# The middle of a mixture-of-slots layer on one core: the norm of the second half re-ordered, and attention pieces set between two halves of a tile

## The chip, the core and the metric

The kernel runs on one core of a Trainium2 chip. The core has a matrix engine (TensorE, PE in the profile; its weight loads are the row PEld), VectorE (DVE), ScalarE (ACT), GpSimd (POOL) and SyncE (SP), whose queue issues most of the DMAs. The metric is the time of one launch in microseconds (us), lower is better, as the median over several runs. All arithmetic is in float32; one float32 matmul of the program is two instructions on PE.

## The reference, cut to what matters

The input x is 4096 tokens of 256 values. Four layers follow one another, each with a layer norm ahead and a residual sum behind: causal attention with 16 heads (a), a soft mixture of experts, another causal attention (b), and the same mixture again with the same weights. The change is in the mixture, which is run twice:

```python
logits = (jnp.einsum('tzd,ed->tze', x, phi_w) + phi_b).reshape(t, z, n, p)  # 64 experts, 32 slots
D = jax.nn.softmax(logits, axis=3)       # over the slots of an expert
C = jax.nn.softmax(logits, axis=2)       # over the experts
X_tilde = jnp.einsum('tznp,tzd->npd', D, x)          # 2048 slots of 256 values
X_tilde = jnp.clip(X_tilde, -33000.0, 65000.0)
mu = jnp.mean(X_tilde, axis=-1, keepdims=True)
var = jnp.mean(jnp.square(X_tilde - mu), axis=-1, keepdims=True)
X_tilde = (X_tilde - mu) * jax.lax.rsqrt(var + LN_EPS)
X_tilde = jnp.tanh(X_tilde)
Y_tilde = jnp.einsum('npd,ndH->npH', X_tilde, expert_w) + expert_b[:, None, :]
Y = jnp.einsum('tznp,npH->tzH', C, Y_tilde)
```

## The kernel before

A mixture layer (`_Experts.run`) has three stages.

**The sweeps.** The 2048 slots are cut into two halves h = 0 and 1 of 1024, and each half sweeps over the 32 token tiles t of 128 tokens, 64 steps in all. A step computes the logits two steps ahead (`logits`: matmuls into the PSUM buffers `lg`, of which there are three, the sum with the bias on DVE at L786, the maximum at L791, a subtraction on POOL at L794, the exponential on ACT at L797), divides one step ahead by the sum of the exponentials (`divide`: a reduction on DVE at L807, a reciprocal at L808, a product on POOL at L809) and adds eight PE instructions into four PSUM banks `acc`. At the end of a half the four banks are clipped into `xt` (DVE, L985). The raw logits go to DRAM (`ld`), for the third stage.

**The norm and the experts of a half.** Groups of 512 slots, numbered n = 0 to 3 (0 and 1 are the first half, 2 and 3 the second), pass three steps. `centre` gets the mean with four PE instructions in one PSUM bank, subtracts it on DVE (two instructions, L701) and squares on ACT (L703). `spread` gets the variance with 16 PE instructions, its root on ACT (L716), and on DVE a reciprocal (L717) and a diagonal matrix (L718). `squash` multiplies with two PE instructions and two on DVE (L730), and takes the tanh on ACT (L731). `product(ec)` then multiplies 128 slots with their experts' weights (16 PE instructions) and adds the bias on DVE (L743); ec = 0 to 7 is the first half, 8 to 15 the second. All these use `net.bank()`, one PSUM bank in this layer. For the first half the steps are hung beside the second half's sweep (`net.beside` runs one of the queue `net.side` per call). For the second half nothing is left to hang them beside: they stand between the sweeps and the combination, written out by hand.

**The combination.** For each tile t the softmax over the experts is needed with the slots on the partitions. `load_l` brings the logits back, `begin` computes the exponentials (POOL L826, ACT L829), `quarter` or `sums` their sum on DVE (four reductions, L856, or one, L845) and `inverse` the reciprocal, with a copy on ACT (L841). `turn_r` transposes the reciprocals on PE and copies them out on ACT (L872, the tile `r`); `turn` transposes the exponentials on PE, 16 transposes in four PSUM buffers' worth, each scaled by `r` on DVE into `lT` (L884). `weigh(t, lo, hi)` is the matmul with the experts' results `ys`, two PE instructions for each ec of the range, 32 for a full tile. `ended` adds the residual (DVE, L901). The tiles 0 and 1 are begun in the last steps of the sweeps (the table `ahead`, by step) and turned there. In the first mixture layer, pieces of attention b's projections (scalings of x on ACT, transposes, matmuls with an ACT copy at L172 and a DVE subtraction at L173) are called with `net.beside(3)` at the end of an iteration, from t = 7 on. At the end of t = 2 attention b's weights are fetched by DMAs from ACT's queue, and at the end of t = 6 and 10 `net.roots` takes a root on ACT (L99) for the norm of the next four tiles.

**What sets the order.** PE instructions stand in the order of the program. On the other engines a list scheduler of the language places an instruction when its own model finds it ready, except where it is wrapped in `pin` (`tc.keep_in_program_order`): that puts it behind the one instruction that was written just before it on its engine. If that one is itself free, the pinned one can move up with it. DMAs of this layer on the SP queue are pinned too. Every engine then works through its stream in order.

Weights: `load_w(ec)` fetches 1 MB of expert weights; 8 to 10 and 14, 15 go to three buffers, 11, 12, 13 to the views 1, 2, 0 of `net.zone`, which the sweeps have used until then (view 0 holds the exponentials of tile 0). `load_b(1)` fetches the second half's bias into the buffer `ebt`, which holds the exponentials of tile 1 until they are turned.

Of the kernel before, what the change touches and what calls it, by code (L numbers as in the profile page):

```python
# [10 lines left out]
F32 = mybir.dt.float32  # L11
# [8 lines left out]
P = 128  # L20
# [22 lines left out]
class _Net:  # L43
# [28 lines left out]
    def bank(self):  # L72
        return self.banks.tile([P, 512], F32, name="bank")
# [533 lines left out]
class _Experts:  # L607
# [28 lines left out]
    def run(self):  # L636
# [10 lines left out]
        with ExitStack() as ctx:  # L647
# [44 lines left out]
            wview = lambda k: net.zone[:, ts(k, E)].rearrange("p (n c h) -> p n c h", n=4, c=2)  # L692
            sqs = {}

            def centre(n):
                xs = xt[:, :, ts(n, 512)]
                mu = net.bank()
                for d in range(2):
                    mm(mu, mean, xs[:, d, :], start=d == 0, stop=d == 1)
                for d in range(2):  # L700
                    nc.vector.tensor_tensor(xs[:, d, :], xs[:, d, :], mu, ALU.subtract)  # L701
# [4 lines left out]
            def spread(n):  # L706
                sq = sqs[n]
                var = net.bank()
# [7 lines left out]
                nc.scalar.activation(r, var[:, 0:4], AF.Sqrt, bias=net.eps)  # L716
                nc.vector.reciprocal(r, r)  # L717
                nc.vector.tensor_tensor(  # L718
                    sq[:, 0, :].rearrange("p (k e) -> p k e", k=4),
                    _bc(net.ident.unsqueeze(1), [P, 4, P]), _bc(r.unsqueeze(2), [P, 4, P]),  # L720
                    ALU.mult,
                )


            def squash(n):
                xs = xt[:, :, ts(n, 512)]
                rs = net.bank()
                mm(rs, one, sqs[n][:, 0, :], start=True, stop=True)
                for d in range(2):
                    nc.vector.tensor_tensor(xs[:, d, :], xs[:, d, :], rs, ALU.mult)  # L730
                nc.scalar.activation(xs, xs, AF.Tanh)  # L731

            def product(ec, bank=net.bank):
                w = ews.pop(ec)
                y = bank()[:, 0:D]
                for j in range(4):
                    for c in range(2):
                        mm(
                            y[ds(32 * j, 32), :], xt[:, c, ds(ec * P + 32 * j, 32)],
                            w[:, j, c, :], start=c == 0, stop=c == 1,  # L740
                        )
                h, e = ec // NC2, ec % NC2
                nc.vector.tensor_tensor(ys[h][:, e, :], y, ebs[h][:, e, :], ALU.add)  # L743
                if ec < NC2:
                    load_w(ec + 3)

# [187 lines left out]
            for k in range(8):  # L934
                ahead[21 + k] = lambda k=k: quarter(k // 4, k % 4)
            ahead[29] = lambda: [maxima(t) for t in range(2, 4)]
            logits(*seq[0])
            logits(*seq[1])
            divide(*seq[0])
            for n, (h, t) in enumerate(seq):  # L940
                if t == 0:
                    acc = [
                        [pa.tile([P, 512], F32, name=f"acc{d}{n2}") for n2 in range(2)]
                        for d in range(2)
                    ]
                if n + 2 < len(seq):
                    logits(*seq[n + 2])
                if n + 1 < len(seq):
                    divide(*seq[n + 1])
                if n < len(seq) - 2:  # L950
                    net.beside(3)
                else:
                    assert not net.side and not net.urgent and not net.agenda
                if h == 1 and t in ahead:
                    ahead[t]()
                if n == len(seq) - 2:

                    nctx.close()
                    pools["lT"] = pool("fc_t", 2)
                    pools["l"] = pool("fc_l", 1)  # L960
                    pools["e"] = pool("fc_w", 1)
                    load_l(2)
                    turn_r(0, first)
                    turn(0, first)
                    begin(2)
                    for k in range(3):
                        load_w(NC2 + 3 + k, wview((1, 2, 0)[k]))
                    load_l(3)
                if n == len(seq) - 1:
                    turn_r(1, first)  # L970
                    turn(1, first)
                    load_b(1)
                ef = es.pop((h, t)).rearrange("p n s -> p (n s)")
                for n2 in range(2):
                    for d in range(2):
                        mm(
                            acc[d][n2], x[:, t, ts(d, P)], ef[:, ts(n2, 512)],
                            start=t == 0, stop=t == NT - 1,
                        )
                if h == 0:  # L980
                    net.beside(3)
                if t == NT - 1:
                    for n2 in range(2):
                        for d in range(2):
                            nc.vector.tensor_scalar(  # L985
                                xt[:, d, ds(h * EH + n2 * 512, 512)], acc[d][n2],
                                -33000.0, 65000.0, ALU.max, ALU.min,
                            )
# [14 lines left out]
            pools["t"] = pool("fc_p", 3, space=PSUM)  # L1003
            pools["o"] = pool("fc_o", 2, space=PSUM)
            two = pool("fc_x", 1, space=PSUM)
            weigh(0, 0, NC2)
            centre(2)
            centre(3)
            spread(2)
            spread(3)  # L1010
            weigh(1, 0, NC2)
            squash(2)
            squash(3)
            for ec in range(NC2, NEC):
                product(ec, (net.bank, lambda: two.tile([P, 512], F32, name="bank2"))[ec % 2])
                if ec < NC2 + 2:
                    load_w(ec + 6)
                if ec < NC2 + 4:
                    quarter(2, ec - NC2)
            turn_r(2)  # L1020
            begin(3)
            rctx.close()
            pools["e"] = pool("fc_w2", 3, side="right")
            pools["l"] = pool("fc_l2", 2, side="right")
# [1 line left out]
            for t in range(NT):  # L1026
                if t + 4 < NT:
                    load_l(t + 4)
                if t > 0:
                    ended(t - 1)  # L1030
                    if t + 3 < NT:
                        begin(t + 3)
                if t == 0:
                    weigh(0, NC2, NEC)
                if 2 <= t + 1 < NT:
                    turn(t + 1)
                if t > 0 and out is None:
                    net.stats(t - 1)
                if t + 4 < NT:
                    maxima(t + 4)  # L1040
                if 4 <= t + 2 < NT:
                    sums(t + 2)
                if t > 0:
                    weigh(t, NC2 if t == 1 else 0, NEC)
                if 4 <= t + 2 < NT:
                    turn_r(t + 2)
                if t == 0:
                    sums(3)
                    turn_r(3)
# [107 lines left out]
```

## Time and profile before

| | |
|---|---|
| median of 3 runs | 5242.63 us (5239.64 to 5249.16) |
| profiled execution, its time | 5241.35 us |
| profiled execution, its span | 5239.3 us |
| mean granted clock of PE | 0.982 |
| first mixture layer in the trace | its last sweep product ends near 2296 us, its combination runs to 2654 us |
| second mixture layer in the trace | its last sweep product ends near 4915 us, its combination runs to the end of the span |

Times are microseconds from the start of the span. A timeline row gives start, duration, engine, line, operation, what it writes and reads, the count of instructions merged in the row, and in brackets how long the engine sat idle before the row and what ended that. A row of stretches gives, for a stretch, its length, the busy time of the engines with their counts, then the granted PE clock (1.00 is full speed), the busy share of the DMA engines and the GB/s they moved.

### The profile page before, as it was taken

The numbers are of one execution on the slowest core, as the hardware profiler recorded it, in microseconds if no ns is written. First come the engines' busy times: TensorE is split into PE (matmuls) and PEld (weight loads), VectorE is DVE, ScalarE is ACT, GpSimd is POOL, SyncE is SP. The second block draws the span as 40 slices with busy tenths as digits, with TensorE's granted clock in tenths as the row PEclk, the third lists the DMA queues.
The fourth block names the chain that finished last, engine by engine and source line by source line (L and its number), as shares of the span: only waits on it lengthen the run. The fifth ranks groups of instructions, "written<-read, shape, count | busy, mean of one in ns | idle before, by whom it ended". The sixth has DMA issues, their size and how long they took to land.

```text
span 5239.3 us, 79442 instructions
## 1 busy us (share of the span) xinstructions
PE 5025.7 (96%) x29936; PEld 2683.4 (51%) x29936; DVE 4141.6 (79%) x7790; ACT 2633.1 (50%) x3108; POOL 1157.2 (22%) x1084
## 2 busy tenths in 40 slices
PE   7999999999999999989989999999999999999899
PEld 4444454445455344447754444545444553444488
DVE  5688989898989388767756889888889893787687
ACT  3466676766667622113224666766666676211132
POOL 3211100000000255534412111000000002555353
PEclk8999999999999999999999999999999999999999
DMA  6433222121121013433444332222121210134343
GB/s 252 140 107 127 67 73 68 61 67 61 59 64 53 32 78 104 148 127 114 144 175 144 107 127 67 72 68 64 64 64 57 64 53 31 77 105 147 122 148 111
DMA packets 266160, 499.16 MB, mean 95 GB/s; under 512 B 44944, under 2 KB 109968, under 8 KB 258096
## 3 DMA queue, kind: packets, MB, share of 16 engines
q1 hardware_dynamic: 260544, 485.57, 28.0%
q10 hardware_dynamic: 4896, 7.87, 0.4%
q8 instruction: 235, 3.85, 0.3%
q14 instruction: 149, 1.22, 0.1%
q0 software_dynamic: 336, 0.66, 0.1%
HBM read 336.73 MB, written 156.76 MB: 94 GB/s over the span
## 4 chain that ended last, share of the span: by engine, by line
PE 75%; DVE 11%; POOL 5%; issue 3%; ACT 3%; DMA 2%; SPq 0%; DVEq 0%; POOLq 0%; ACTq 0%
PE o L67 26%; PE bank L67 22%; PE sc L67 17%; PE acc L67 4%; DVE mx L386 4%; PE lg L67 4%; DVE junk L380 2%; POOL e L794 2%; PE ps L70 2%; POOL e L809 2%; ACT e L797 1%; DVE l L786 1%; ACT pb L462 1%; POOL e L826 1%; DMA zone<-ld 0%
## 5 line engine op out<-in xcount | busy, mean ns | idle before, releaser
L462 ACT ACTIVATE pb<-sc 128x1024 f32<-128x1024 f32 (+3 forms) x2304 | 2070.1, 950 | 1104.0 <-PE sc L67 1101.3
L386 DVE TENSOR_REDUCE mx<-bank 128x1 f32<-128x512 f32 x3584 | 2225.4, 682 | 179.5 <-PE bank L67 174.8
L67 PE MATMUL bank<-k,q 64*128 64x512 f32 (+3 forms) x4608 | 1354.7, 454 | 71.0 <-DVE mx L386 29.8
L67 PEld LDWEIGHTS bank<-k,q 64*128 64x128 f32 x4608 | 669.4, 186 | 1178.1 <-DVE mx L386 777.6
L67 PE MATMUL o<-pb,va 128*32 128x512 f32 (+3 forms) x9216 | 1160.4, 575 | 3.1 <-POOL pb L466 2.8
L67 PE MATMUL sc<-q,k 64*128 64x512 f32 (+3 forms) x4608 | 991.9, 391 | 9.6 <-ACT pb L462 9.2
L67 PE MATMUL sc<-qm,one 64*128 64x512 f32 (+3 forms) x4608 | 951.8, 378 | 0.0
L466 POOL TENSOR_SCALAR_AFFINE_SELECT pb<-pb 128x256 f32<-128x256 f32 x512 | 204.8, 407 | 2281.3 <-ACT pb L462 2275.5
L380 DVE CUSTOM_DVE_ANT_0 junk<-bank,maskw 128x128 bf16<-128x128 f32 (+3 forms) x1024 | 502.5, 491 | 258.9 <-PE bank L67 150.6
L67 PEld LDWEIGHTS sc<-q,k 64*128 64x128 f32 x4608 | 512.2, 187 | 138.2 <-ACT pb L462 98.9
L67 PEld LDWEIGHTS sc<-qm,one 64*128 64x128 f32 x4608 | 528.9, 187 | 67.7
L67 PE MATMUL acc<-e,x 128*128 128x512 f32 x1024 | 473.1, 605 | 19.3 <-POOL e L809 14.7
L797 ACT ACTIVATE e<-e 128x1024 f32<-128x1024 f32 x128 | 135.2, 1057 | 694.6 <-POOL e L794 694.6
L67 PE MATMUL lg<-zone,xnT 128*128 128x512 f32 x1024 | 463.3, 594 | 4.4 <-DVE l L786 3.8
L67 PE MATMUL o<-ys,lT 128*128 128x256 f32 x2048 | 464.9, 386 | 1.6 <-DVE xt L985 1.6
L67 PEld LDWEIGHTS o<-ys,lT 128*128 128x128 f32 x2048 | 392.6, 194 | 56.1 <-DVE xt L985 3.2
L826 POOL TENSOR_TENSOR e<-l,mc 128x1024 f32<-128x1024 f32 x120 | 281.3, 2365 | 319.5 <-DMA l<-ld 209.9
L67 PEld LDWEIGHTS o<-pb,va 128*32 128x32 f32 x9216 | 183.2, 108 | 290.6 <-issue 265.7
L67 PEld LDWEIGHTS acc<-e,x 128*128 128x128 f32 x1024 | 192.6, 193 | 265.5 <-issue 215.9
L809 POOL TENSOR_TENSOR e<-e,s 128x1024 f32<-128x1024 f32 x128 | 244.8, 1912 | 370.0 <-DVE s L808 348.5
L67 PEld LDWEIGHTS lg<-zone,xnT 128*128 128x128 f32 x1024 | 192.2, 190 | 245.7 <-issue 217.9
L807 DVE TENSOR_REDUCE s<-e 128x32 f32<-128x1024 f32 x128 | 156.1, 1219 | 155.2 <-ACT e L797 154.6
(122 smaller groups left out, 3208.4 us busy)
## 6 DMA issues: line engine op xcount, KB each, us to landing
k<-ak SPq DMA_DIRECT2D x144, 512.0 KB
k<-bk SPq DMA_DIRECT2D x144, 512.0 KB
ld<-l SPq DMA_DIRECT2D x128, 512.0 KB
l<-ld SPq DMA_DIRECT2D x60, 1024.0 KB
w<-in_L_ffn_expert_w_dram SPq DMA_DIRECT2D x26, 1024.0 KB
q<-aq SPq DMA_DIRECT2D x32, 512.0 KB
rb<-dd SPq DMA_DIRECT2D x64, 256.0 KB
q<-bq SPq DMA_DIRECT2D x32, 512.0 KB
```

The lines of the kernel that those rows point to most:

```text
L67: self.tc.keep_in_program_order(self.nc.tensor.matmul(*a, **k))
L70: self.tc.keep_in_program_order(self.nc.tensor.transpose(o, i, self.ident))
L380: nc.vector.tensor_tensor_reduce(out=junk[:, 0:w], in0=scs[h2][:, 0:w], in1=maskw[:, QB - w : QB], scale=1.0, scalar=-3e38, op0=ALU.add, o ...
L386: nc.vector.tensor_reduce(m, scs[h2], AX.X, ALU.max)
L462: nc.scalar.activation(pb[:, :, off:QB], sc[:, :, off:QB], AF.Exp)
L466: nc.gpsimd.affine_select(out=d, in_=d, compare_op=ALU.is_ge, fill=0.0, base=0, pattern=[[0, 2], [1, P]], channel_multiplier=-1,)
L786: nc.vector.tensor_tensor(lf[:, ts(n, 512)], lg, phb[:, ds(h * EH + n * 512, 512)], ALU.add)
L794: nc.gpsimd.tensor_tensor(e, l, _bc(m.unsqueeze(2), [P, NH, SLOT]), ALU.subtract)
L797: nc.scalar.activation(ef, ef, AF.Exp)
L807: nc.vector.tensor_reduce(s, e, AX.X, ALU.add)
L809: nc.gpsimd.tensor_tensor(e, e, _bc(s.unsqueeze(2), [P, NH, SLOT]), ALU.mult)
L826: nc.gpsimd.tensor_tensor(e[:, ns, :], l, _bc(cms[t].unsqueeze(1), [P, NH, SLOT]), ALU.subtract)
```

## The change

It has five parts. (1) `centre`, `spread` and `squash` take the PSUM bank as an argument, and their DVE instructions, those of `product` and the clipping L985 are pinned. (2) `turn_r(0)` and `turn_r(1)` move up into the sweep, to its steps t = 26 and 30 of the second half; the transposes of the tiles 0 and 1 move down, out of the last two steps. (3) Behind the sweeps, the two groups of the second half are taken side by side, group 2 in the one bank and group 3 in a second bank that before only the products used in turn, with `turn(1)` between `centre` and `spread`, `turn(0)` between `spread` and `squash`, and `weigh(0, 0, 8)` behind `squash`; the weights and the bias that need the freed buffers are fetched behind those steps. (4) `begin(3)` moves from behind the products to ahead of them, and `weigh(1, 0, 8)` is cut in four pieces between pairs of products. (5) In the combination a tile's `weigh` is cut in two halves, and from t = 7 on in the first mixture layer `net.beside(3)` is called between the halves and not at the iteration's end.

```diff
-            def centre(n):
+            def centre(n, bank=net.bank):
                 xs = xt[:, :, ts(n, 512)]
-                mu = net.bank()
+                mu = bank()
...
-                    nc.vector.tensor_tensor(xs[:, d, :], xs[:, d, :], mu, ALU.subtract)
+                    pin(nc.vector.tensor_tensor(xs[:, d, :], xs[:, d, :], mu, ALU.subtract))
...
-                nc.vector.tensor_tensor(ys[h][:, e, :], y, ebs[h][:, e, :], ALU.add)
+                pin(nc.vector.tensor_tensor(ys[h][:, e, :], y, ebs[h][:, e, :], ALU.add))
...
             ahead[29] = lambda: [maxima(t) for t in range(2, 4)]
+            ahead[26] = lambda: (quarter(1, 1), turn_r(0, first))
+            ahead[30] = lambda: turn_r(1, first)
...
                     load_l(2)
-                    turn_r(0, first)
-                    turn(0, first)
                     begin(2)
-                    for k in range(3):
-                        load_w(NC2 + 3 + k, wview((1, 2, 0)[k]))
-                    load_l(3)
-                if n == len(seq) - 1:
-                    turn_r(1, first)
-                    turn(1, first)
-                    load_b(1)
+                    for k in range(2):
+                        load_w(NC2 + 3 + k, wview(1 + k))
...
             two = pool("fc_x", 1, space=PSUM)
+            load_l(3)
+            banks = (net.bank, lambda: two.tile([P, 512], F32, name="bank2"))
+            centre(2, banks[0])
+            centre(3, banks[1])
+            turn(1)
+            load_b(1)
+            spread(2, banks[0])
+            spread(3, banks[1])
+            turn(0)
+            load_w(NC2 + 5, wview(0))
+            squash(2, banks[0])
+            squash(3, banks[1])
+            begin(3)
             weigh(0, 0, NC2)
-            centre(2)
-            centre(3)
-            spread(2)
-            spread(3)
-            weigh(1, 0, NC2)
-            squash(2)
-            squash(3)
             for ec in range(NC2, NEC):
-                product(ec, (net.bank, lambda: two.tile([P, 512], F32, name="bank2"))[ec % 2])
+                product(ec, banks[ec % 2])
                 if ec < NC2 + 2:
                     load_w(ec + 6)
                 if ec < NC2 + 4:
                     quarter(2, ec - NC2)
+                if ec % 2:
+                    weigh(1, ec - NC2 - 1, ec - NC2 + 1)
             turn_r(2)
-            begin(3)
...
+                beside = self.attention is not None and t > 6
                 if t > 0:
-                    weigh(t, NC2 if t == 1 else 0, NEC)
+                    lo = NC2 if t == 1 else 0
+                    half = lo + (NEC - lo) // 2
+                    weigh(t, lo, half)
+                    if beside:
+                        net.beside(3)
+                    weigh(t, half, NEC)
                 if 4 <= t + 2 < NT:
                     turn_r(t + 2)
...
-                    if t > 6:
-                        net.beside(3)
```

More of the change, by code (lines that the diff above doesn't have):

```diff
@@ L700, in centre, with spread @@
                 for d in range(2):
-                    nc.vector.tensor_tensor(xs[:, d, :], xs[:, d, :], mu, ALU.subtract)
+                    pin(nc.vector.tensor_tensor(xs[:, d, :], xs[:, d, :], mu, ALU.subtract))
                 sqs[n] = ewk.tile([P, 2, 512], F32, name="sq")
                 nc.scalar.activation(sqs[n], xs, AF.Square)
-            def spread(n):
+            def spread(n, bank=net.bank):
                 sq = sqs[n]
-                var = net.bank()
+                var = bank()
                 for k in range(4):
@@ L716, in spread @@
                 nc.scalar.activation(r, var[:, 0:4], AF.Sqrt, bias=net.eps)
-                nc.vector.reciprocal(r, r)
-                nc.vector.tensor_tensor(
+                pin(nc.vector.reciprocal(r, r))
+                pin(nc.vector.tensor_tensor(
                     sq[:, 0, :].rearrange("p (k e) -> p k e", k=4),
@@ L721, in spread, with squash @@
                     ALU.mult,
-                )
-            def squash(n):
+                ))
+            def squash(n, bank=net.bank):
                 xs = xt[:, :, ts(n, 512)]
-                rs = net.bank()
+                rs = bank()
                 mm(rs, one, sqs[n][:, 0, :], start=True, stop=True)
                 for d in range(2):
-                    nc.vector.tensor_tensor(xs[:, d, :], xs[:, d, :], rs, ALU.mult)
+                    pin(nc.vector.tensor_tensor(xs[:, d, :], xs[:, d, :], rs, ALU.mult))
                 nc.scalar.activation(xs, xs, AF.Tanh)
@@ L984, in run @@
                         for d in range(2):
-                            nc.vector.tensor_scalar(
+                            pin(nc.vector.tensor_scalar(
                                 xt[:, d, ds(h * EH + n2 * 512, 512)], acc[d][n2],
                                 -33000.0, 65000.0, ALU.max, ALU.min,
-                            )
+                            ))
                     if h == 0:
```

## The prediction

> **What bounds the kernel now.** I read the page's first part, the stretches around the two mixture layers, and the engines' timelines there. PE is busy in 96% of the span, so only what shortens PE's work, its waits or its slow clock counts.
>
> ```profile
> PE 5025.7 (96%) x29936; PEld 2683.4 (51%) x29936; DVE 4141.6 (79%) x7790; ACT 2633.1 (50%) x3108; POOL 1157.2 (22%) x1084
> 2357.50:2653.90 296.40, 274.16 (x1436) 236.00 (x1437) 211.69 (x286) 80.83 (x129) 118.89 (x51) 0.98 0.34 115
> 4962.19:5239.30 277.11, 273.86 (x1485) 240.52 (x1484) 206.73 (x234) 75.24 (x113) 130.45 (x56) 0.99 0.40 131
> 2273.39:2342.82 69.43, 49.73 (x272) 31.32 (x270) 33.72 (x53) 14.46 (x20) 18.12 (x9) 0.83 0.48 153
> 4893.60:4962.02 68.42, 47.97 (x272) 30.84 (x270) 33.62 (x52) 14.69 (x20) 15.77 (x8) 0.85 0.46 143
> ```
>
> The last two rows are the passage from sweep to combination (end of the third-last sweep product to `turn_r(3)`): PE is idle for some 20 us of each, with a granted clock of 0.83 to 0.85. The second row, the second layer's combination, is full; the first layer's lacks 22 us. The PE timeline of the second passage names the waits:
>
> ```profile
> 4901.77 1.12 PE L70 MATMUL lg<-ident,zone 128*128 128x128 f32 x4 [3.63 <-ACT r L872]
> 4904.71 5.10 PE L67 MATMUL acc<-e,x 128*128 128x512 f32 x8
> 4911.70 3.60 PE L67 MATMUL acc<-e,x 128*128 128x512 f32 x8
> 4922.90 1.99 PE L67 MATMUL bank<-xt,mean 128*128 128x512 f32 x4 [1.38 <-DVE xt L701]
> 4928.93 3.58 PE L67 MATMUL bank<-mean,sq 128*128 128x1 f32 x16 [0.66 <-ACT rx L716]
> 4932.37 6.70 PE L67 MATMUL o<-ys,lT 128*128 128x256 f32 x16
> 4953.91 1.09 PE L67 MATMUL bank<-w,xt 128*32 128x256 f32 x16 [1.87 <-DMA w<-in_L_ffn_expert_w_dram]
> 4962.02 0.33 PE L70 MATMUL rT<-ident,s 128*128 128x128 f32 x1 [3.31 <-ACT s L841]
> ```
>
> Step by step one bank serves both groups, so group 3 waits for group 2's DVE work; and 6.70 us for sixteen instructions that take 3.72 elsewhere is PE at half clock after waits. In the first layer's combination (PE, then ACT):
>
> ```profile
> 2425.41 0.65 PE L70 MATMUL ps<-ident,e 128*128 128x128 f32 x4 [4.32 <-DVE lT L884]
> 2425.90 8.76 PE L67 MATMUL o<-ys,lT 128*128 128x256 f32 x32
> 2517.14 0.66 PE L70 MATMUL ps<-ident,e 128*128 128x128 f32 x4 [1.02 <-DVE lT L884]
> 2464.33 1.06 ACT L829 ACTIVATE e<-e 128x1024 f32<-128x1024 f32 x1 [1.26 <-POOL e L826]
> 2465.29 0.25 ACT L872 COPY r<-rT 128x128 f32<-128x128 f32 x1
> ```
>
> The copy of `r` for tile t+1 stands behind exponentials of tile t+3 that are late, DVE cannot scale, PE waits. 9.13 us is an undisturbed iteration (2381.68 to 2390.82).
>
> **The passage, step by step.** Removed from the last two sweep steps: 32 transposes and two `turn_r`. `acc` of t = 31 then waits only for its divided exponentials: L809 starts at 4903.35 and takes 1.91, so 4905.26 and not 4911.70, a gain of 6.4 (first layer 2285.04 against 2292.58, 7.5). PE idles ahead of t = 30's `acc` (free at 4893.6 plus `turn_r(1)`, data at 4898.48); that is no loss, as the chain through DVE, POOL and ACT sets 4905.26.
>
> From there to `turn_r(3)` PE must do: `acc` 3.44; two `centre` 3.44; 32 transposes 3.9; two `spread` 3.8; two `squash` 1.72; `weigh(0)`'s first half 3.45; eight products at 1.02, 8.2; `weigh(1)`'s four pieces 3.45; `turn_r(2)` 0.1; `weigh(0)`'s second half 3.45. Sum 35.0. What is still waited for, by laying DVE's pinned order beside it (clips 0.7 each behind `acc`, two subtractions 1.28 per group, four scalings 2.5 per tile, 1.0 per `spread`, 1.28 per `squash`): the fourth transposes of each tile need a scaling first, 0.7 and 0.8; a product waits 0.3 for its bank; `turn_r(3)` waits 1.0 for `sums(3)` (3.6 plus 0.35 plus the copy, from the last bias sum on, beside 3.45 of `weigh`). Sum 2.8. The ACT steps hide: squares (1.06 each) under `turn(1)`, roots and a table load (1.28) under `spread(3)` and `turn(0)`, both tanh under `weigh(0)`; uncovered, tanh would cost 2.1. So 37.8, against 50.3 (4911.70 to 4962.02) and 50.2: gains of 12.5 and 12.4.
>
> In the second layer `turn(2)` behind this runs at a slow clock (3.47 for 2.1 us of transposes), 1.5 more. **Passages: 6.4 + 12.5 + 1.5 + 7.5 + 12.4 = 40.3.**
>
> Moved at no cost: `begin(3)`. Its exponentials wait today behind `turn_r(2)`'s copy on ACT, hence the 3.31; placed ahead of the products, POOL has 4.7 us of work some 10 us early. Its SP loads keep their order except that the weights of ec = 13 go behind `load_l(3)` and `load_b(1)`; the product needs them some 11 us after they are issued, and the pair of 1 MB loads behind product 9 landed within 5.9 and 8.9 us (4945.01 issued, 4950.9 and 4953.9 used). The same pair has 7.5 and 8.3 us in the new order: 0 to 1.5 us a layer, I take 0.
>
> `turn_r(0)` in the sweep holds an `lg` buffer until its ACT copy, which is pinned behind t = 28's exponential: 13 us with two buffers in place of three. PE then waits some 2.1 us at the next logits, but the sweep's period of 7.97 there is set by the DVE-POOL-ACT chain (PE works 6.9 of it), and the evictions come 7 us after the matmuls. Cost 0; at most 2.1 a layer.
>
> The pins on the first half's steps: those DVE rows already stand behind L808 of their step (L701 at 2062.69 after L808 at 2062.42). 0.
>
> **The combination of the first layer.** Four matmul pieces (t = 17 to 20) make iterations of 11.73; their PE work is 1.72, so 0.87 each is the DVE subtraction ahead of the scalings; between the halves it lies under 3.45 us of `weigh`: 3.5. Three transposes' pieces wait 0.42, 0.58, 0.59 where 0.15 is normal: 1.1. The piece at t = 31 spares the 1.40 that the next one waits for its bank. The order of the pins matters more: the exponentials of `begin` are pinned behind the ACT instruction written last, which is a free scaling of x wherever `beside` stood there, so they slip ahead of the copy of `r`. With `beside` ahead of `turn_r`, they are held behind it. That removes the stalls at t = 9 (4.32, and 1.69 of slow clock, less 0.15), 13 (2.13 + 1.69 - 0.15), 23 (1.75) and 27 (2.04): 13.3. The stalls at t = 3 and 7 stay (a weight DMA and `roots` break the pin there), and at t = 11 `roots` now is last where a transposed piece held the order: one new stall, 3.5 as at t = 7. **Combination: 3.5 + 1.1 + 1.4 + 13.3 - 3.5 = 15.8.** The second layer has no pieces: its two halves cost 0.
>
> **The clock.** After the 1.98 us wait of t = 7 the granted clock is halved, after 2.04 at t = 27 the 32 instructions take 7.07, full speed:
>
> ```profile
> 2402.00:2404.00 2.00, 2.00 (x7) 1.62 (x6) 2.00 (x5) 0.00 (x0) 0.14 (x1) 0.58 0.50 209
> 2572.00:2574.00 2.00, 1.39 (x9) 1.29 (x10) 2.00 (x4) 0.00 (x0) 0.00 (x0) 1.00 1.02 434
> ```
>
> So a wait near 2 us may or may not halve it; the new waits of at most 1.0 I count at full clock. One dip in each passage would cost 1.7 (8.76 against 7.07). [...]
>
> **Sum.** 40.3 + 15.8 = 56.1 off 5241.35 gives 5185.3; the median lies 1.3 above the profiled execution: 5187. Without any remaining wait (2 x 2.8) and without the new stall (3.5), 5178. With a dip per passage (3.4), late weights (3.0) and held buffers (4.2), 5197.
>
> **Rivals.** (A) The stalls move and do not go: the pins do not do what they say, since what held `r` back was a late logits load, and the load is late wherever it stands. For it: after each stall the next iteration has none, as loads had time. Against: the second layer, same loads, no pieces, has no stall at all. It gives 40.3 + 6.0 - 3.5 = 42.8, so 5200. (B) The weights become the wait: three 1 MB loads and 1 MB of bias in some 15 us, where waits of 1.87 and 2.17 for weights stand today. At 5 us a layer, 5197. (C) Slower: the sweep. Its second half carries 14 side steps a layer whose DVE rows are now pinned. If the scheduler sets each directly behind L808 and so ahead of the two evictions L786, DVE waits there for the side step's matmuls: 2.3 us, from L808 at 2115.08 to the product's PE end near 2117.7, less what is idle. 28 steps at 2.3 are 64, and 56 is won: 5250. From 2.0 a step it is slower. Against: pins hold back only the pinned, evictions stay free to go first, as today (L743 at 2112.45, behind both).
>
> **Chances.** The forecast 0.66, with its own range 5178 to 5197; A 0.15; B 0.09; C 0.10, its weak form between 5200 and 5230 counted there. The range 5172 to 5212 takes in A and B and some of C. A measurement of this kernel tells 0.2%, 10.5 us, from no change. Faster 0.90, same 0.03, slower 0.07.
>
> **What would show it.** Right: `acc` of t = 31 starts at L809's end; the passage takes some 50 us from the end of t = 29's `acc` to `turn_r(3)`; no PE wait over 1.5 us in it after `acc`; in the first layer's combination stalls at t = 3, 7 and 11 only and iterations of 10.9 at t = 17 to 20. Wrong: PE waits for `w`, a sweep period over 8.1 us at its side steps, or rows of `r` still behind late exponentials.

## The result and the profile after

The changed kernel takes 5180.21 us (median of 4 runs, 5169.84 to 5184.01); the kernel before, run beside it, 5242.33. The ratio on record is 0.9886, 95% interval 0.9871 to 0.9901 (the medians alone give 0.9882). The forecast was 5187, from 5172 to 5212. The profiled execution took 5181.23, its span is 5179.5: 59.8 less than before. Total lines of the page:

```profile
PE 5005.9 (97%) x29936; PEld 2674.3 (52%) x29936; DVE 4142.0 (80%) x7790; ACT 2632.8 (51%) x3108; POOL 1157.3 (22%) x1084
```

The instructions are the same in number, and so is the work on DVE, ACT and POOL. PE is busy 19.8 us less with as many instructions, so at a better clock (granted 0.986 on the mean, 0.982 before), and 40 us of its idle time are gone. Where these us lie is shown by a table of stages, cut at the same PE instructions in every trace: *head* runs from the end of the third-last sweep product (`acc` of t = 29) to the start of `acc` of t = 31, *passage* from there to `turn_r(3)`, *combination* from there to the last matmul of the last tile's `weigh`. The change does not touch the code of attention a and b, but for one matmul piece (1.7 us) that moved out of the start of attention b into the first combination; in the sweeps it sets `turn_r(0)` and the pins.

| us | attention a | sweeps 1 | head 1 | passage 1 | combination 1 | attention b | sweeps 2 | head 2 | passage 2 | combination 2 |
|---|---|---|---|---|---|---|---|---|---|---|
| before | 1793.4 | 480.0 | 19.2 | 50.2 | 310.9 | 1758.5 | 481.4 | 18.1 | 50.3 | 273.6 |
| after | 1785.3 | 480.0 | 11.7 | 38.4 | 297.1 | 1759.4 | 480.9 | 11.2 | 39.5 | 272.5 |

Stretches of the trace after (length, then busy time of PE, PEld, DVE, ACT and POOL, granted clock, DMA share, GB/s): first passage with its head, the second, the first combination.

```profile
2265.20:2315.34 50.14, 42.76 (x272) 26.87 (x271) 34.19 (x52) 14.20 (x19) 16.58 (x8) 0.93 0.69 212
4852.70:4903.42 50.72, 44.34 (x272) 29.28 (x271) 33.96 (x52) 13.71 (x19) 15.03 (x7) 0.90 0.60 190
2315.34:2612.70 297.36, 286.93 (x1522) 246.87 (x1523) 222.76 (x305) 87.61 (x137) 131.17 (x56) 0.99 0.36 124
```

PE's idle time in a passage with its head (the length less PE's busy time) fell from 20 to 7 and 6 us. The PE timeline of the second passage shows what is left:

```profile
4863.94 3.70 PE L67 MATMUL acc<-e,x 128*128 128x512 f32 x8 [1.38 <-POOL e L809]
4867.48 3.60 PE L67 MATMUL bank<-xt,mean 128*128 128x512 f32 x8
4870.91 1.47 PE L70 MATMUL ps<-ident,ebt 128*128 128x128 f32 x12
4873.05 0.66 PE L70 MATMUL ps<-ident,ebt 128*128 128x128 f32 x4 [0.67 <-DVE lT L884]
4873.54 5.56 PE L67 MATMUL bank<-mean,sq 128*128 128x1 f32 x32
...
4903.42 0.33 PE L70 MATMUL rT<-ident,s 128*128 128x128 f32 x1 [0.35 <-ACT s L841]
```

`acc` of t = 31 now starts when L809 ends (4863.94, L809 at 4863.88). The two `centre` and the two `spread` stand in one row each: group 3 no longer waits for group 2. `turn(1)`, the third and fourth row, covers the squares, and 0.35 us is all that `turn_r(3)` waits, where it waited 3.31. But the 32 instructions of `spread` take 5.56 us, where the first layer's take 3.63, without a wait in them.

The first combination, PE:

```profile
2413.24 0.65 PE L70 MATMUL ps<-ident,e 128*128 128x128 f32 x4 [2.40 <-DVE lT L884]
...
2474.12 1.88 PE L67 MATMUL bank<-zone 128*128 128x512 f32 x4
```

The piece of the last row lies between two halves of a tile, 3.62 us each, and nothing waits; the tile's first half starts at 2470.67, the next tile's at 2481.52, an iteration of 10.85. The stalls at t = 3 and 7 are still there (waits of 1.78 and 2.18, before 2.03 and 1.98). The stall of 2.40, at t = 11, is new. Its cause stands on ACT:

```profile
2410.77 1.06 ACT L829 ACTIVATE e<-e 128x1024 f32<-128x1024 f32 x1 [1.27 <-POOL e L826]
...
2412.22 0.24 ACT L872 COPY r<-rT 128x128 f32<-128x128 f32 x1
```

The copy of `r` is again behind a late exponential. PE's waits for DVE's scalings over the first combination, before and then after (total, times, longest):

```profile
PE ps L70 <- DVE lT L884: 21.5, 23, 4.3
```

```profile
PE ps L70 <- DVE lT L884: 7.4, 10, 2.4
```

### The profile page after: what moved, and what is told of

Read it like the earlier page. It is cut to its first block, busy times and chain, and to the rows that moved or that the text cites. A ratio compares the mean times of both kernels' runs of the same rounds, so it can differ in the third digit from the quotient of the medians.

```text
span 5179.5 us, 79445 instructions
## 1 busy us (share of the span) xinstructions
PE 5005.9 (97%) x29936; PEld 2674.3 (52%) x29936; DVE 4142.0 (80%) x7790; ACT 2632.8 (51%) x3108; POOL 1157.3 (22%) x1084
## 4 chain that ended last, share of the span: by engine, by line
PE 77%; DVE 10%; POOL 4%; issue 3%; ACT 3%; DMA 2%; SPq 0%; DVEq 0%; POOLq 0%; ACTq 0%
PE o L67 27%; PE bank L67 22%; PE sc L67 17%; PE acc L67 5%; PE lg L67 4%; DVE mx L386 4%; DVE junk L380 2%; POOL e L794 2%; PE ps L70 2%; POOL e L809 1%; ACT e L797 1%; DVE l L786 1%; ACT pb L462 1%; PE bank L70 0%; DMA zone<-ld 0%
## 5 line engine op out<-in xcount | busy, mean ns | idle before, releaser
L67 PE MATMUL acc<-e,x 128*128 128x512 f32 x1024 | 472.1, 604 | 26.3 <-POOL e L809 21.8
L809 POOL TENSOR_TENSOR e<-e,s 128x1024 f32<-128x1024 f32 x128 | 244.8, 1912 | 369.0 <-DVE s L808 349.4
```

Source lines behind the costliest of these rows:

```text
L67: self.tc.keep_in_program_order(self.nc.tensor.matmul(*a, **k))
L809: nc.gpsimd.tensor_tensor(e, e, _bc(s.unsqueeze(2), [P, NH, SLOT]), ALU.mult)
```

## The experiments

The theory: three things that add up, the side-by-side norm with the transposes between its steps (passages), the two moves of `turn_r` (heads), and in the first combination the place of `beside` ahead of `turn_r`, which orders the exponentials behind the copy of `r`, and inside the tile, which hides the piece's DVE subtraction. The main rival: the stalls of the combination come from late loads and would only move.

Stages of the profiled runs:

| us | head 1 | passage 1 | combination 1 | head 2 | passage 2 | combination 2 |
|---|---|---|---|---|---|---|
| only the passage | 11.7 | 38.7 | 310.4 | 11.2 | 41.2 | 273.4 |
| only the mid tile | 18.7 | 50.2 | 298.6 | 17.5 | 50.4 | 272.9 |
| only the order | 19.0 | 50.1 | 305.9 | 19.0 | 49.8 | 272.7 |
| no pins | 11.7 | 38.9 | 293.7 | 11.3 | 39.7 | 272.6 |
| one bank | 11.7 | 44.2 | 295.2 | 11.2 | 43.1 | 272.6 |
| turns back | 18.6 | 39.2 | 298.7 | 18.8 | 39.3 | 273.3 |
| `begin(3)` late | 11.7 | 41.0 | 298.1 | 11.7 | 41.4 | 273.6 |
| roots inside | 11.2 | 39.1 | 288.7 | 11.3 | 39.8 | 273.7 |
| roots inside, again | 11.3 | 40.3 | 288.9 | 11.3 | 40.5 | 272.5 |
| changed kernel, again | 11.3 | 39.8 | 296.3 | 11.7 | 38.6 | 272.6 |
| `turn(0)` early | 12.2 | 38.0 | 287.8 | 12.0 | 39.2 | 273.5 |
| wide between | 11.3 | 42.7 | 287.4 | 11.3 | 40.0 | 273.1 |

**Only the passage.** The changed kernel with part (5) undone:

```diff
-                    weigh(t, lo, half)
-                    if beside:
-                        net.beside(3)
-                    weigh(t, half, NEC)
+                    weigh(t, NC2 if t == 1 else 0, NEC)
...
+                    if t > 6:
+                        net.beside(3)
```

> The changed kernel with the combination's loop as it was before: a tile's matmul in one piece and the attention pieces at the iteration's end. Theory (the two places add up): both passages keep their gain of some 20 us each, and the first layer's combination is as long as before, from the first turn_r(3) to the end of the last full tile some 13 us longer than in the changed kernel, with PE waits of about 2 us or more for the scalings near t = 3, 7, 9, 13, 23 and 27; time about 5195 to 5203. Rival (the half tiles do nothing, what was gained in the combination follows from the passage, which lets the loads run ahead): the combination is as short as in the changed kernel, time about 5180 to 5187.

5201.29 us, ratio 0.9931 (0.9915 to 0.9947). The heads and passages gain what they gain in the whole change, but for the second passage, which is 1.7 us longer: half clock lasts longer there (`squash` takes 3.19 us, in the changed kernel 1.88). The first combination gains nothing. PE waits there 21.4 us for DVE's scalings, as before.

**Only the mid tile.** The kernel before with part (5) alone:

```diff
-                    weigh(t, NC2 if t == 1 else 0, NEC)
+                    weigh(t, lo, half)
+                    if beside:
+                        net.beside(3)
+                    weigh(t, half, NEC)
...
-                    if t > 6:
-                        net.beside(3)
```

> The kernel of before with only the half tiles in the combination and the attention pieces between them. Theory: the passages stay at 69 and 68 us, the first layer's combination is 13 to 16 us shorter, with stalls left at t = 3, 7 and 11; time about 5227 to 5230. Rival (the gain in the combination needs the passage): within 4 us of before, 5238 to 5242.

5218.86 us, ratio 0.9964 (0.9953 to 0.9975). The first combination is 12.3 us shorter, 14.0 without the piece that moved into it, and keeps three long waits, at t = 3, 7 (2.35 and 2.16) and, on PE's timeline, at t = 11:

```profile
2431.41 0.66 PE L70 MATMUL ps<-ident,e 128*128 128x128 f32 x4 [2.46 <-DVE lT L884]
```

The two ratios multiply to 0.9895, against 0.9886 for the whole: the parts add up.

**Only the order.** The kernel before; the exponentials from tile 6 on must be issued behind the last copy of `r`, and `beside` stays at the iteration's end:

```diff
-                pin(nc.scalar.activation(e[:, ns, :], e[:, ns, :], AF.Exp))
+                if t > 5:
+                    with tc.issue_after(last["r"].ins):
+                        nc.scalar.activation(e[:, ns, :], e[:, ns, :], AF.Exp)
+                else:
+                    pin(nc.scalar.activation(e[:, ns, :], e[:, ns, :], AF.Exp))
...
-                pin(nc.scalar.copy(rts[t], rT))
+                last["r"] = pin(nc.scalar.copy(rts[t], rT))
```

> The kernel of before with one edge added: from tile 6 on the two exponentials of begin are issued behind the last copy of r on ACT. Tiles stay whole, the pieces stay at the iteration's end. Theory (the order on ACT makes the long stalls, the place of the pieces only the small ones): the waits at t = 3, 7, 9, 13, 23 and 27 are all gone, 4.3 + 1.7, 2 x (2.0 + 1.7), 2.1 + 1.7, 1.8 and 2.0, some 20 us; the four matmul pieces still make iterations of 11.7 us; time about 5222. Rival (the late logits load is the cause and the order only shows it): the waits stay or move to the sums, less than 6 us shorter than before.

5231.03 us, ratio 0.9986 (0.9975 to 0.9997): far less than the 20 us that were expected. The six waits at t = 3, 7, 9, 13, 23 and 27 are gone, as the theory said: these iterations take 9.0 to 9.1 us each. But the four iterations with a matmul piece got waits of their own. The timelines of PE, ACT, DVE and POOL around the second piece (in this kernel L828 and L833 are the subtraction and the exponential of `begin`, L890 is the scaling; L172 is the piece's copy, L173 its subtraction):

```profile
2505.78 1.11 PE L70 MATMUL ps<-ident,e 128*128 128x128 f32 x4 [5.68 <-DVE lT L890]
```

```profile
2502.55 1.06 ACT L833 ACTIVATE e<-e 128x1024 f32<-128x1024 f32 x1 [1.25 <-POOL e L828]
2503.51 0.57 ACT L172 CAST zone<-bank 128x512 fp32r<-128x512 f32 x1
```

```profile
2504.11 0.69 DVE L173 TENSOR_TENSOR zone<-bank,zone 128x512 fp32r<-128x512 f32 x1 [8.35 <-ACT zone L172]
```

```profile
2497.85 4.66 POOL L828 TENSOR_TENSOR e<-l,mc 128x1024 f32<-128x1024 f32 x2 [11.72 <-DMA l<-ld]
```

The piece's ACT copy now stands behind the held exponentials, its DVE subtraction waits 8.35 us for that copy, and the scalings stand behind the subtraction, from 2505.05 on. The four waits, 1.76, 5.68, 2.23 and 6.04, cost most of what the order had won: the combination is 5.0 us shorter. That number alone does not end the rival, which gave it less than 6: what the held exponentials wait for is still POOL, and POOL the load. So a late load makes a stall where a short copy that others need stands behind the exponentials; whether the order alone is enough to end it is tested by "roots inside" below. The mid tile is worth more than the 3.5 us of its DVE subtraction, too: it also brings the piece's copy ahead of the exponentials, and the four iterations that take 12.47 to 18.47 us here take 10.85 in the changed kernel.

**No pins.** The changed kernel without the pins of part (1), six in all, each like this:

```diff
-                    pin(nc.vector.tensor_tensor(xs[:, d, :], xs[:, d, :], mu, ALU.subtract))
+                    nc.vector.tensor_tensor(xs[:, d, :], xs[:, d, :], mu, ALU.subtract)
```

> The changed kernel without the new pins: the clips, the DVE instructions of centre, spread, squash and the products' bias sums are free again, all else as changed. Theory (the pins only fix an order that readiness gives anyway): acc of the last sweep step to turn_r(3) stays at 38 to 40 us in both layers, sweeps 480 to 482. Rival (without them the scheduler puts the scalings of the transposes or the quarter sums ahead of the norm's steps): 41 to 45 us there.

5180.35 us in one run; head and passage as with them, sweeps 480.9 and 480.5. The pins fix an order that the list scheduler takes anyway. Neither a gain nor the price of rival C. The first combination, where none of these pins stands, is 3.4 us shorter in this profile: PE waits at t = 7 and 11 as before (2.27 and 2.26), but behind both the 32 instructions of `weigh` take 7.07 us, full clock, and not 8.76.

**One bank.** Group 3 uses the bank of group 2:

```diff
-            centre(3, banks[1])
+            centre(3, banks[0])
...
-            spread(3, banks[1])
+            spread(3, banks[0])
...
-            squash(3, banks[1])
+            squash(3, banks[0])
```

> The changed kernel with one PSUM bank for both groups in centre, spread and squash; the products still take two. Theory (the second bank spares the wait for the other group's reader): group 3 waits again 1.4 us in centre, 0.7 in spread and 1.4 in squash, so the stretch from the last sweep product to turn_r(3) is 41 to 43 us, not 38.4 and 39.5. Rival (what matters is what stands between the steps; the bank is free in time): under 1 us more.

5188.03 us in one run. The passages are 5.8 and 3.6 us longer, 44.2 and 43.1 where 41 to 43 was expected. The old waits are back on PE's timeline, and the second `spread` runs at half clock behind them (3.41 us for 1.85):

```profile
2287.66 1.98 PE L67 MATMUL bank<-xt,mean 128*128 128x512 f32 x4 [1.38 <-DVE xt L701]
2303.60 1.12 PE L67 MATMUL bank<-sq,one 128*128 128x512 f32 x2 [1.38 <-DVE xt L730]
```

**Turns back.** Both `turn_r` and both `turn` at their old place in the sweep, the norm still side by side:

```diff
-            ahead[26] = lambda: (quarter(1, 1), turn_r(0, first))
-            ahead[30] = lambda: turn_r(1, first)
...
+                    turn_r(0, first)
+                    turn(0, first)
...
+                    turn_r(1, first)
+                    turn(1, first)
...
-            turn(1)
...
-            turn(0)
```

> The changed kernel with turn_r and the transposes of tiles 0 and 1 back in the last two sweep steps, none between the norm's steps; banks, pins, begin(3) and the cut weigh as changed. Theory: the wait ahead of the last sweep product is back (18 to 19 us from the third-last product's end, not 11 to 12), and the stretch from there to turn_r(3) has 3.9 less of transposes and 3 more of waits, 36 to 38 us: 5 to 6 us a layer longer in sum. Rival (the transposes are only moved, PE has to do them anyway): the sum of both stretches stays at 50 to 51 us.

5194.52 us in one run. Head and passage together take 57.8 and 58.1 us against 50.1 and 50.7: 7.7 and 7.4 longer, where 5 to 6 was expected. The head takes its 7 us back; the passage has 32 transposes less and is not shorter, since `spread` and what follows run without the cover of the transposes, and at half clock (3.58 us for 1.95; granted 0.68 on the mean from 2286 to 2302):

```profile
2290.30 3.58 PE L67 MATMUL bank<-mean,sq 128*128 128x1 f32 x16 [1.30 <-ACT sq L703]
...
2297.34 4.80 PE L67 MATMUL o<-ys,lT 128*128 128x256 f32 x16
```

**`begin(3)` late**, behind the products as before:

```diff
-            begin(3)
             weigh(0, 0, NC2)
...
             turn_r(2)
+            begin(3)
```

> The changed kernel with begin(3) back behind turn_r(2). Theory (its exponentials wait on ACT behind the copy of r for tile 2, the sum of tile 3 behind them): PE waits some 3.3 us for turn_r(3) again, not 0.4, the stretch is 41 to 43 us, and the second layer may run the next transposes at half clock (1.4 more in its combination). Rival (the sum waits for DVE, which is busy with the products' sums until then): under 1 us more.

5182.19 us in one run. The passages are 2.6 and 1.9 us longer. The wait of before returns, and the transposes behind it take 3.44 us, not 2.10:

```profile
2319.53 0.48 PE L70 MATMUL rT<-ident,s 128*128 128x128 f32 x1 [3.17 <-ACT s L841]
```

**Roots inside.** The changed kernel; what broke the pins at t = 2, 6 and 10 goes between the halves too, ahead of `turn_r`:

```diff
                         net.beside(3)
+                    if self.attention is not None:
+                        if t == 3:
+                            self.attention.load_weights()
+                        if t in (6, 10):
+                            b = (t - 6) // 4
+                            net.roots(4 * b, 4 * b + 4)
+                            net.side.extend(self.attention.pieces(b, fast=True, values=False))
...
-                    if t == 2:
-                        self.attention.load_weights()
-                    if t in (6, 10):
...
```

> The changed kernel, with the root for the next tiles' norm (t = 6 and 10) and the fetch of attention b's weights (now t = 3) also put between the two halves of a tile, so ahead of the copy of r. Theory: the last three stalls of the combination, t = 3 (1.8), 7 (2.2 + 1.7) and 11 (2.4 + 1.7), are gone, 9 to 10 us shorter than the changed kernel, every iteration without a piece at 9.1 us. Rival (the stalls are due to something that recurs every four tiles, such as the four residual buffers or the load): they appear one or two tiles later, no gain.

5166.21 us, ratio 0.9869 (0.9852 to 0.9885), by the median better than the changed kernel. The first combination is 8.4 us shorter, somewhat less than the 9 to 10 that were expected, and the three stalls are gone. PE's waits for scalings there (total, times, longest):

```profile
PE ps L70 <- DVE lT L884: 0.8, 5, 0.2
```

That shows what made the last three stalls: an instruction of ACT's queue, here a weight fetch and two roots, that is written between the copy of `r` and the exponentials. It also ends the rival. The loads stand where they stood and are still waited for (22 times by POOL, 100.1 us in all; 24 times and 114.5 us in the changed kernel), and no stall comes back at a later tile, here or in the three more kernels below that have this.

Three kernels measured beside each other show whether this holds and whether the passage has more to give. The changed kernel again:

> The changed kernel once more, beside the two that follow, on one chip: 5175 to 5185 us, 1.0 to 1.3% under the kernel before. Its stages with unchanged code (attention a and b) are expected to differ from the first profile of it by up to 10 us, since so far they lay between 1780.8 and 1793.4 us and between 1752.5 and 1763.6 us.

5177.76 us, ratio 0.9885 (0.9869 to 0.9902). The roots inside, again:

> The changed kernel with the roots at t = 6 and 10 and the weights' fetch at t = 3 set between the halves of the tile, again, to see whether its gain holds. If the three stalls are the cause: 8 us less than the changed kernel in the first layer's combination, about 5170. If the first measurement was only a lucky run: within 3 us of the changed kernel.

5168.55 us, ratio 0.9871 (0.9855 to 0.9888); the combination is 7.4 us shorter than in the changed kernel beside it, with no wait for a scaling over 0.5. The gain holds in its stage; in the totals the intervals of the two kernels overlap. And on top of it `turn(0)` moved between the last two sweep products, where PE waits 1.4 us:

```diff
+                if n == len(seq) - 1:
+                    turn(0, first)
+                    load_w(NC2 + 5, wview(0))
...
-            turn(0)
-            load_w(NC2 + 5, wview(0))
```

> The kernel above, with the 16 transposes of tile 0 and the load of the weights for ec = 13 moved from between spread and squash to between the last two sweep products, where PE waits 1.4 us for t = 31's divided exponentials and DVE is idle for 3.3 us. If PE's work behind acc of t = 31 is what sets the passage: its 16 transposes (1.95) and two waits of 0.7 leave it, so the passage is 2 to 3.5 us shorter in each layer, the head at most 1 longer, and the time 2 to 6 us under the kernel above, about 5164. Rival: the fourth transposes wait for a scaling there too and acc of t = 31 starts later by as much as is won, or the steps that the transposes parted now wait for DVE (spread to squash); then the sum of head and passage stays within 1 us of 50.3 a layer and the time within 3 us.

5170.63 us, ratio 0.9876 (0.9861 to 0.9891): no gain to be seen beside the 5168.55. Head and passage sum to 50.2 and 51.2, against 51.6 and 51.8 (50.3 and 51.1 in the first profile of the roots inside). Most of it is eaten by what the transposes had covered, as the rival had it: `squash` now waits for DVE, and takes 3.55 us for its four instructions instead of 1.88.

```profile
2294.21 3.55 PE L67 MATMUL bank<-sq,one 128*128 128x512 f32 x4 [1.07 <-DVE rx L717]
```

**Wide between**, on the kernel with the roots inside: is it the waits that halve the clock in the passage, or that PE does only transposes and one-column matmuls there?

```diff
             turn(1)
             load_b(1)
+            weigh(1, 0, 2)
             spread(2, banks[0])
+            weigh(1, 2, 4)
             spread(3, banks[1])
+            weigh(1, 4, 6)
             turn(0)
+            weigh(1, 6, NC2)
...
-                if ec % 2:
-                    weigh(1, ec - NC2 - 1, ec - NC2 + 1)
```

> What halves the clock in the norm of the second half? In all traces of the changed kernel and of the one with the roots inside, the stretch from turn(1) to squash (some 11 us) runs partly at half clock, although PE waits there no longer than 0.7 us at a time. From the start of the acc of t = 31 to the start of weigh(0) those traces show 18.5 or 19.9 us, of which 1.5 and 3.1 are half clock. Here, on the kernel with the roots inside, the eight steps of weigh(1, 0, 8) stand in four pairs behind turn(1), spread(2), spread(3) and turn(0) and no longer between the products: the same instructions, 3.45 us of matmuls over 256 columns set among the transposes and the matmuls of one column. Theory (the clock falls where PE does only transposes and one-column matmuls for several us, busy or not): no half clock from turn(1) to squash, and 20.4 us from acc to weigh(0), 16.9 without the pairs. Rival (the waits of 0.7 us, or the 1.4 us ahead of acc, do it): the dip stays and the stretch is 22.0 to 23.4 us. The products then stand alone and will wait for their two banks or for DVE, some 2 to 4 us a layer by the bias sums (0.68) and quarters (0.94) behind each, so the time is expected within 4 us of the kernel with the roots inside, 5164 to 5172, either way.

The second layer has no half clock from `turn(1)` to `squash`: 20.2 us from `acc` to `weigh(0)`, as the theory said, with the same wait of 0.67 in it. PE's timeline there, the transposes behind that wait and one `spread` at full speed:

```profile
4871.96 0.65 PE L70 MATMUL ps<-ident,ebt 128*128 128x128 f32 x4 [0.67 <-DVE lT L884]
...
4873.32 1.84 PE L67 MATMUL bank<-mean,sq 128*128 128x1 f32 x16
```

The first layer still has a short dip (21.8 us; a `weigh` pair takes 2.06 for 1.03), between the two expectations. One stretch in two ran clean, where none of the eight others traced in the changed kernel and with the roots inside did: it speaks for the theory and does not settle it. The rival had a second wait, the 1.4 us ahead of `acc`, and this was not the same: it is 0.51 ahead of the clean stretch and 1.38 ahead of the other. Against that rival speaks one passage of "roots inside, again", where that wait is 0.80 and the dip costs the full 3.1. The time, 5180.57, ratio 0.9881 (0.9863 to 0.9898), is not better, as the products, now alone, wait for their banks and weights (0.96 and 1.65 us at the worst). The expected 5164 to 5172 was missed.

## Why the prediction was right, step by step

| term, us | predicted | measured between the two profiles |
|---|---|---|
| heads | 7.5 + 6.4 | 7.5 + 6.9 |
| passages | 12.4 + 12.5 | 11.8 + 10.8 |
| `turn(2)` behind the second | 1.5 | 1.1 |
| first combination, without the piece at t = 31 | 14.4 | 15.5 (310.9 - 297.1, and 1.7 of work that moved in) |
| wait behind the piece at t = 31 | 1.4 | gone, but not to be seen in attention b's time |

**Heads.** Right: `acc` waits for L809 alone.

**Passages.** 37.8 was forecast; 38.4 and 39.5 came, and 39.8 and 38.6 when the same kernel was profiled again. Two terms were off, in opposite directions. The waits after the start of `acc` were put at 2.8 and are 1.6 and 1.0: no product waits for its bank, and `turn_r(3)` waits 0.37 and 0.35 instead of 1.0. The clock was put at full speed, and it was not: in the second layer `spread` takes 5.56 for 3.63 and `turn(0)` 3.29 for 2.1, 3.1 us in all; in the first a dip from the end of `turn(0)` into `squash` costs 1.5. Without both, 35.3 remains in either layer of the predicted 35.0 of PE work. The step that failed is "the new waits of at most 1.0 I count at full clock": the waits are indeed no longer than 0.67, and the clock fell all the same. A dip of 1.7 a passage stood in the range only; 1.5 and 3.1 came. That the passages came out within 2 us of the forecast is in part luck, as the shorter waits paid for some two thirds of the dips.

**Costs taken as nothing.** The weights: waits of 0.27 us in the first layer and none in the second, within the 0 to 1.5. `begin(3)`: right, and left behind it costs 2.6 and 1.9. The `lg` buffer that `turn_r(0)` holds: the wait for it is there, 1.95 us at the next logits in both layers, and the sweeps take 480.0 and 480.9 against 480.0 and 481.4, so it is hidden. The pins: nothing. The halves of `weigh` in the second layer: nothing.

**Combination.** Right in its places: stalls at t = 3, 7 and 11 only, 10.85 at t = 17 to 20. The waits for scalings fell by 14.1. The new stall was 2.40 and some 1.7 of slow clock, 4.1 for the predicted 3.5. What outweighs that was not foreseen: the iteration at t = 3, which was to stay as it was, takes 10.93 us and not 12.82, with a wait of 1.78 for 2.03 and no slow clock behind it (the 32 instructions of `weigh` take 7.07 for 8.43). Most of that is luck with the clock: the iteration takes 10.63 us in the second profile, too, but 12.71 with the turns back and 12.92 with `begin(3)` late.

**The rivals.** A fell with the roots inside: no wait for a scaling over 0.5 us, with the loads where they were. The order alone took the old stalls away, but made new ones behind the same loads. B: the weights are waited for 0.27 us. C: neither with nor without pins does the sweep change.

**The sum.** In its place the change brought 14.4 + 22.6 + 1.1 + 15.5 = 53.6 us of the predicted 56.1. The two profiles lie 59.8 apart: attention a, whose code is the same, took 8.1 less in the profile after, the sweeps 0.5 less, and attention b, counted with the moved piece, 2.6 more. Without that the profiled execution would have been 5187.7, 2.4 over the 5185.3 that the prediction gave it. The medians of the two measurements lie 62.1 and 59.6 apart, also more than the 53.6; where the rest of that comes from is not shown. So the change itself brought a little less than was forecast; that the median still came out 6.8 us under the forecast is luck.

**The clock.** `acc` of t = 30 ran into a dip: its eight instructions take 5.40 us for 3.60 behind a wait of 3.65, with 0.50 granted from 4859 to 4861. It costs nothing, as `acc` of t = 31 still waits 1.38 us behind it for L809. But the same trace has a dip where the longest wait in the ten us ahead is 0.67 (stretches of the second passage, columns as above, the granted clock third from the end):

```profile
4872.00:4874.00 2.00, 1.33 (x13) 1.09 (x12) 2.00 (x4) 1.55 (x2) 2.00 (x2) 1.00 0.00 0
...
4876.00:4878.00 2.00, 2.00 (x11) 2.00 (x11) 0.87 (x2) 0.00 (x0) 0.01 (x1) 0.50 1.11 238
...
4882.00:4884.00 2.00, 2.00 (x8) 1.04 (x7) 1.94 (x4) 0.00 (x0) 0.00 (x0) 1.00 0.16 42
```

PE is marked busy there all the time, with one-column matmuls and transposes, and still gets half the clock for some 7 us. Nor does the length of a wait decide: in the second profile of the changed kernel two waits of 2.33, at t = 7 and 11, are followed by 7.07 us and by 8.76 us for the same 32 instructions.

So idle time alone does not explain the half clock of these runs. What PE does in such a stretch, here only transposes and one-column matmuls, would fit, and "wide between", with matmuls over 256 columns set between them and no half clock in one layer of two, leans that way, but does not show it.

## What to carry to other kernels

When an engine in program order waits, look at what was written just before the pinned instruction: one free neighbour (a root, a scaling, a DMA's issue) between a copy and the work that should stand behind it opened a stall of 2 to 4 us, and moving the neighbour closed it. Put side work between two halves of a long run of matmuls rather than at a seam, so that both its copy and its subtraction have cover (12.3 us off the first combination here), and use work that is ready (transposes) to fill the steps of a chain through other engines, with a bank for each of two groups (7.7 and 7.4 us here, with the moves of `turn_r`, and 5.8 and 3.6 for the second bank). Do not count the clock by the waits alone: some 11 us of transposes and one-column matmuls, with no wait over 0.67, cost 1.5 to 3.1 us a time in the changed kernel here. That this comes of what PE does there is likely and not settled.

## What the runs showed of the hardware that was not expected

Half clock came to a PE that was busy, as above, and where it fell changed from run to run of the same program: in the first profile of the changed kernel the first layer's `spread` ran at full clock and the second's did not (3.63 and 5.56 us), in the second profile it was the other way round (5.37 and 3.63).

Code that nobody changed differs more between runs than some of these parts are worth. Attention a took from 1780.8 to 1793.4 us over all profiles; two profiles of the same kernel (the roots inside) have 1791.3 and 1784.5. Most of that difference has built up in the first 260 us: from 130 to 260 PE does 702 instructions in the one run and 739 in the other, at a granted clock of 0.91 and 0.95, first run, then the second:

```profile
130.00:260.00 130.00, 120.17 (x702) 59.67 (x704) 86.56 (x229) 60.35 (x85) 28.13 (x49) 0.91 0.42 140
```

```profile
130.00:260.00 130.00, 120.86 (x739) 60.27 (x739) 91.19 (x246) 64.68 (x90) 28.16 (x49) 0.95 0.41 142
```

So a gain of a few us is better read from its own stage of a profile than from the total.
